# Long VectorE and GpSimd steps cut into two to four parts, and one planned duration corrected, in a planned four-layer transformer

## The chip, the core and the metric

The kernel runs on one core of a Trainium2 chip. The core has a matrix engine (TensorE, PE in the profile), three engines for elementwise work (VectorE is DVE, ScalarE is ACT, GpSimd is POOL) and a queue that starts transfers (SyncE, SP). Each engine takes its instructions strictly in the order in which the program lists them, and waits for other engines at semaphores. The metric is the device time of one execution in microseconds (us); lower is better.

## The reference

An input of 16 sequences of 256 tokens with 128 features passes through four layers in fp32. Every layer adds an attention and then a feed-forward block to x, each behind a layer norm:

```
x = x + attn_l(layernorm(x));  x = x + ffn_l(layernorm(x))       # l = 0..3
L0 attn: 16 heads of 64, l2-normed q and k, distance bias, 2 null keys;  ffn: gelu, 512 hidden
L1 attn: q of 16 heads of 8, one shared k and v, causal;  ffn: silu(x w1) * (x w2), two gelu layers of 512, w3
L2 attn: 16 heads of 64, no mask, biases;  ffn: 8 experts, each token goes to the one with the largest gate logit
L3 attn: 16 heads of 8, causal window of 128;  ffn: mix with the previous token, sigmoid(xr Wr) * (relu(xk Wk)^2 Wv)
```

## The kernel before

All of x stays in SBUF as eight tiles (xg), each for two batches, with tokens on the partitions. Layers run one after the other, but the work of neighbouring batches and layers is interleaved.

The order is not written by hand. The kernel records *steps* with `step(engine, p, ns, emit, r, w, m)`: p is a rank (smaller is earlier in the program's own order), ns the duration that the planner assumes, r, w and m are what the step reads, writes, and changes in place. Two steps that name the same value under m follow each other. `Plan.run` then plays the steps against a model of the engines: it starts with the engine that is free first, takes among the steps that could start within 40 ns the one with the smallest rank, and emits its instructions. A step is never interrupted, so a long one holds its engine for its whole planned duration. The planned durations thus decide the order of the instructions, but not how long they take on the chip. A step for two engines ("DP" is VectorE or GpSimd, "AD" is ScalarE or VectorE) has a planned duration for each and goes to the one that would end it earlier. Tile buffers (the homes: eight PSUM banks "t", "r", "probs", "pT" and so on) are handed out in the same run. SP's queue carries the loads of weights and expert rows, GpSimd's the scatters and gathers.

The places that matter here, with their lines:

- `layernorm` (455 to 482): statistics on VectorE (lines 464 and 465, two row blocks each), eps and power -1/2 on GpSimd (lines 469 and 436), and the application (line 477, two instructions), which in layer 0 is always on VectorE and otherwise "DP".
- `narrow_keys` (line 596): in layers 1 and 3 one GpSimd instruction spreads the keys of a batch over four masked copies.
- `narrow_out` (lines 683 to 687): the attention output of layers 1 and 3 is divided by the sums, for two halves z of the tokens, then turned on TensorE and projected.
- `feed1` (lines 1021 and 1022): two gating instructions for each of four blocks of 128 hidden features.
- `through` (lines 1111 to 1114): once, the bias of v is carried through the output matrix, in eight instructions.
- `Experts.gate` (lines 1197 to 1220): for each two batches of layer 2, the gate logits, the choice of the expert (`chosen`, six small VectorE instructions), counts on TensorE, and running sums on GpSimd (`running`, four). `place` computes each token's place in its expert's blocks; `scatter` (line 1304) writes 128 normed tokens at a time to DRAM by an indirect transfer from GpSimd's queue.
- `block`: SP loads an expert's weights (line 1316) and 128 rows (line 1317); the rows are turned on TensorE and copied out to a tile bT (lines 448 and 450), and two products, a relu (lines 1334 and 1336) and a bias follow. Experts work in two groups of four tiles of x (eight batches) each; `back` (line 1353) gathers the results once all blocks of a group are written. Layer 3 of the second eight batches can't begin before that.

The matrix products carry line 404 and the transposes line 432, those of the helpers that issue them; copies out of PSUM have line 448 on ScalarE and 450 on VectorE.

Of the kernel before, what the change touches and what calls it, by code (L numbers as in the profile page):

```python
# [12 lines left out]
ALU = mybir.AluOpType  # L13
AX = mybir.AxisListType

P = 128
# [223 lines left out]
def preln_d4_kernel(ctx: ExitStack, tc: tile.TileContext, x_in, vecs, rows, nullk, nullv,  # L240
                    wa0, wlat, wb1, wa2, wex, gatew, wa3, out):
    nc = tc.nc
    PSUM = bass.MemoryType.PSUM
    plan = Plan()
    step, get = plan.step, plan.get
# [188 lines left out]
    def rsqrt(t, n):  # L434

        nc.gpsimd.tensor_tensor(t, t, mhalf[:t.shape[0]].broadcast_to([t.shape[0], n]), ALU.pow)  # L436

    def x_of(b):
        return xg[b // 2][:, (b % 2) * 2:(b % 2) * 2 + 2, :]

    X = [plan.key(f"x{b}") for b in range(B)]
# [14 lines left out]
    def layernorm(b, p, xn, at, times=1, behind=(), eng="DP"):  # L456

        ln, x = get("ln"), x_of(b)  # L460

        def stats(e):
            for i in range(2):
                nc.vector.bn_stats(ln.t[0][:, i, :], x[:, i, :])
                nc.vector.bn_aggr(ln.t[1][:, i, :], ln.t[0][:, i, :])  # L465

        def scale(e):
            if times == 1:
                nc.gpsimd.tensor_scalar(ln.t[2], ln.t[1][:, :, 1], LN_EPS, 1.0, ALU.add, ALU.mult)  # L469
            else:  # L470
                nc.gpsimd.tensor_scalar(ln.t[2], ln.t[1][:, :, 1], 1.0 + LN_EPS, LN_EPS * LN_EPS, ALU.mult, ALU.add)
            rsqrt(ln.t[2], 2)

        def apply(e):
            for i in range(2):
                v = nc.vector if e == "DVE" else nc.gpsimd
                v.tensor_scalar(xn.t[:, (at + i) * D:(at + i + 1) * D], x[:, i, :], ln.t[1][:, i, 0:1],
                                ln.t[2][:, i:i + 1], ALU.subtract, ALU.mult)

        step("DVE", p, 788, stats, r=[X[b]], w=[ln])  # L480
        step("POOL", p, 1070, scale, m=[ln])
        step(eng, p, (520, 620) if eng == "DP" else 520 if eng == "DVE" else 620, apply, r=[X[b], ln] + list(behind), w=[xn])

    def turned(p, xn, nt, gamma=None):

# [105 lines left out]
    def narrow_keys(p, KT):  # L591

        KM = get("K")

        def keys(e):
            nc.gpsimd.tensor_tensor(KM.t[:, :, 0:256], KT.t[:, 0:256].unsqueeze(1).broadcast_to([P, 4, 256]),
                                    owner.unsqueeze(2).broadcast_to([P, 4, 256]), ALU.mult)

        step("POOL", p, 1850, keys, r=[KT, "owner"], w=[KM])
        return KM  # L600

    def narrow_unit(q, b, u, st, mask, mkey):
# [64 lines left out]
    def narrow_out(p, b, st, w_proj):  # L667

        t, o_sb, rs, oT = [get("t"), get("t")], get("small"), get("rs"), st["oT"]

        def turn(e):
            for i in range(4):
                turned_halves(t, 64 * i, oT.t[:, i * P:(i + 1) * P])

        step("PE", p, 250, turn, r=[oT], w=t, mode="S")

        def divided(e):

            o6 = o_sb.t[:, 0:256].rearrange("p (q z g h d) -> p q z g h d", q=2, z=2, g=2, h=4)
            r5 = rs.t.rearrange("p (z q g h) -> p z q g h", z=2, q=2, g=2)  # L680
            for z in range(2):
                t5 = t[z].t[:, 0:256].rearrange("p (s q g r) -> p s q g r", s=2, q=2, g=2)
                nc.vector.reciprocal(r5[:, z, :, :, 0:3], t5[:, 0, :, :, 24:27])
                nc.vector.reciprocal(r5[:, z, :, :, 3:4], t5[:, 1, :, :, 24:25])
                nc.vector.tensor_tensor(o6[:, :, z, :, 0:3, :], t5[:, 0, :, :, 0:24].rearrange("p q g (h d) -> p q g h d", d=8),
                                        r5[:, z, :, :, 0:3].unsqueeze(4).broadcast_to([P, 2, 2, 3, 8]), ALU.mult)
                nc.vector.tensor_tensor(o6[:, :, z, :, 3, :], t5[:, 1, :, :, 0:8],
                                        r5[:, z, :, :, 3:4].broadcast_to([P, 2, 2, 8]), ALU.mult)

        step("DVE", p - 7, 1060, divided, r=t, w=[o_sb], m=[rs])  # L690
        yT = get("small")

        for t2, src, dst in in_halves(p + 1, (o_sb, lambda i: o_sb.t[:, i * P:(i + 1) * P]), 2, lambda: yT.t):
            evac(p + 1, yT, t2, lambda src=src, dst=dst: (dst(), src()), 128)
        y = get("t")

        def project(e):
            for qc in range(2):
                mm(y.t[:, qc * P:(qc + 1) * P], yT.t[:, qc * P:(qc + 1) * P], w_proj)

        step("PE", p + 2, 450, project, r=[yT], w=[y], mode="P")
        add_to_x(p + 2, b, y)
# [10 lines left out]
    first, rank = {}, 0  # L713
# [290 lines left out]
    def feed1(g):  # L1004
        lo = first[1, 2 * g + 1] + 8 + 16
        x, xx = xg[g], [X[2 * g], X[2 * g + 1]]
        xn = get("r")
# [5 lines left out]
        for c in range(4):  # L1013
            pa, pb, th = get("t"), get("t"), get("sq")

            def up(e, c=c, pa=pa, pb=pb):
                mm(pa.t, wt("w1", c * P, P), xnT.t)
                mm(pb.t, wt("w2", c * P, P), xnT.t)

            def gated(e, c=c, pa=pa, pb=pb, th=th):  # L1020
                nc.vector.scalar_tensor_tensor(th.t, th.t, 1.0, pa.t, ALU.add, ALU.mult)
                nc.vector.scalar_tensor_tensor(h[c].t, pb.t, s12[:, c:c + 1], th.t, ALU.mult, ALU.mult)

            p = lo + 6 + c
            step("PE", p, 1724, up, r=[xnT, "w1", f"h2.{g - 1}"], w=[pa, pb], mode="P")
            step("ACT", p - 8, 560, lambda e, c=c, pa=pa, th=th: nc.scalar.activation(th.t, pa.t, AF.Tanh, scale=s1h[:, c:c + 1]),
                 r=[pa, "s1"], w=[th])
            step("DVE", p - 8, 1380, gated, r=[pa, pb, "s1"], m=[th], w=[h[c]])

        def layer(name, sname, src, p):  # L1030
            dst = [get("r") for _ in range(4)]
# [72 lines left out]

    bvo, bps = get("small"), get("t")

    def through(e):
        a = v_at["a2bv"][0]
        for c in range(8):
            wo = wA[:, 3072 + c * D:3072 + (c + 1) * D]  # L1110
            if c == 0:
                nc.vector.tensor_scalar(bvo.t[:, 0:D], wo, vec_sb[:, a:a + 1], None, ALU.mult)
            else:
                nc.vector.scalar_tensor_tensor(bvo.t[:, 0:D], wo, vec_sb[:, a + c:a + c + 1], bvo.t[:, 0:D], ALU.mult, ALU.add)

    step("DVE", first[2, 0] - 12, 1800, through, r=["w2"], w=[bvo])
    step("PE", first[2, 0] - 8, 224, lambda e: mm(bps.t[:, 0:D], ones, bvo.t[:, 0:D]), r=[bvo, "ones"], w=[bps], mode="P")
    step("DVE", first[2, 0] - 8, 200, lambda e: nc.vector.tensor_tensor(row("a2bo"), bps.t[:, 0:D], row("a2bo"), ALU.add), r=[bps], w=["a2bo"])  # L1118

# [48 lines left out]
    class Experts:  # L1168
# [12 lines left out]
        def gate(self, g, lo):  # L1181
# [11 lines left out]
            def chosen(e):  # L1193
# [4 lines left out]
                nc.vector.tensor_reduce(m1, l3, AX.X, ALU.max)  # L1198
                nc.vector.tensor_tensor(l3, l3, m1.unsqueeze(2).broadcast_to([P, 4, 8]), ALU.is_equal)
                nc.vector.scalar_tensor_tensor(l3, l3, -64.0, iota8.unsqueeze(1).broadcast_to([P, 4, 8]), ALU.mult, ALU.add)  # L1200
                nc.vector.tensor_reduce(m2, l3, AX.X, ALU.min)
                nc.vector.tensor_tensor(self.tile("oh")[:, a:a + 4, :], l3, m2.unsqueeze(2).broadcast_to([P, 4, 8]), ALU.is_equal)

            step("PE", lo + 7, 600, logits, r=[xnT], w=[ps], mode="P")
            oh = plan.get(None)
            step("DVE", lo + 5, 1150, chosen, r=[ps, "late"], m=[lg, self.key("oh")], w=[oh])
            pc = get("t")

            def counts(e):
# [7 lines left out]
            def running(e):  # L1217
                sofar = self.tile("sofar")
                for t in range(a, a + 4):
                    nc.gpsimd.tensor_tensor(sofar[:, t + 1, :], sofar[:, t, :], self.tile("ct")[:, 1, t, :], ALU.add)  # L1220

            step("PE", lo + 9, 300, counts, r=[oh], w=[pc], mode="P")
            ct = plan.get(None)
            step("DVE", lo + 3, 131, kept, r=[pc], w=[ct, self.key("ct")])
            step("POOL", lo + 9, 720, running, r=[ct], m=[self.key("sofar")])

        def place(self, g, lo):

# [60 lines left out]
                if last:  # L1289
                    v.tensor_copy(self.tile("owni"), own)  # L1290

            def in_parts(p, times, ops, r, m):

                todo = ops()
                for ns in times:
                    step("DVE", p, ns, lambda e: next(todo, None), r=r, m=m)

            in_parts(lo, (700, 600, 1100), blocks_of, [self.key("sofar")], [self.key("nb")])
            in_parts(lo, (600, 450, 650), places, [self.key("nb"), self.key("oh"), self.key("sofar")], [self.key("ct")])
            in_parts(lo + 1, (700, 1000, 800), owners, [self.key("ct")], [self.key("nb")])  # L1300

        def scatter(self, t, p):
            def f(e):
# [1 line left out]
                    out=ex_rows[self.part], out_offset=bass.IndirectOffsetOnAxis(ap=self.tile("idx")[:, t:t + 1], axis=0),  # L1305
                    in_=self.xn[self.lo + t // 4].t[:, (t % 4) * D:(t % 4 + 1) * D], in_offset=None)

            step("POOL", p, 980, f, r=[self.key("ct"), self.xn[self.lo + t // 4]], m=[self.key("rows")], tail=2500)

        def block(self, j, p):  # L1310
            w, xs, xsT, h, ys = get("w"), get("xs"), get("bT"), get("r"), get("bT")
# [277 lines left out]
```

## Time and profile before

| | |
|---|---|
| median of 3 runs | 2126.34 us (2121.66 to 2129.11) |
| profiled execution, its own time | 2132.18 us |
| its span, first to last instruction | 2130.5 us |
| mean granted TensorE clock | 0.982 of full speed |
| TensorE idle in 0 to 100 us | 14.8 us |
| TensorE idle in 1700 to 2100 us | 39.7 us |

Each line of the groups names a source line, an engine, an operation and its tiles with buffer numbers, then durations in ns. A line of waits says which instruction waited for which, how many us in total, how often, and the longest. In the list of instructions by time, a bracket at the end gives how long the engine had been idle before, and what ended that. A group of scores, exponentials and products of one batch in layer 0 takes some 36 us, in layer 1 some 33, in layer 2 some 34. The four layers lie at about 0 to 600, 570 to 1180, 1130 to 1770 and 1740 to 2130 us.

### The profile page before, as it was taken

To read this page: it belongs to the slowest core of one execution; us is meant where nothing else is said; L and a number is where in the kernel's file an instruction comes from. 1 tells how busy PE (TensorE), PEld (TensorE's weight loads), DVE (VectorE), ACT (ScalarE), POOL (GpSimd) and SP (SyncE) were. 2 spreads that over 40 slices of the span, in tenths; PEclk is the share of its full clock that TensorE was granted. 3 is DMA by queue.
4 is the path that set the end of the run, shared out by engine and by line. 5 is a ranking of instruction groups with operands and counts; after the bars stand their busy time and mean duration, and the time that the engine had idled before them with its cause. 6 is when DMAs were issued, how large, how long until landed. Compare 5 with 4: busy or idle time off the path is not lost.

```text
span 2130.5 us, 86226 instructions
## 1 busy us (share of the span) xinstructions
PE 2030.3 (95%) x34860; PEld 1395.8 (66%) x34860; DVE 1636.7 (77%) x6393; ACT 1660.5 (78%) x4834; POOL 1159.3 (54%) x2157
## 2 busy tenths in 40 slices
PE   7999999999999999999999999999999998998997
PEld 4667777777665444544546677777887775775665
DVE  7999999999887766667665467777676778677997
ACT  6999999998887776767766668877666778677996
POOL 7888888898842121212223346666454974227642
PEclk9999999999999999999999999999999998998999
DMA  5000000000140000000000000000442001441000
GB/s 168 2 2 2 2 2 2 2 2 3 32 61 12 2 3 3 3 3 3 3 3 1 2 4 5 7 7 18 123 122 74 22 7 45 140 146 29 15 8 18
DMA packets 60303, 59.08 MB, mean 28 GB/s; under 512 B 28016, under 2 KB 49024, under 8 KB 59904
## 3 DMA queue, kind: packets, MB, share of 16 engines
q1 hardware_dynamic: 57680, 49.33, 8.3%
q8 instruction: 274, 4.49, 0.9%
q0 software_dynamic: 2048, 4.20, 0.6%
q14 instruction: 125, 1.02, 0.2%
q10 hardware_dynamic: 176, 0.03, 0.0%
HBM read 43.32 MB, written 10.22 MB: 25 GB/s over the span
## 4 chain that ended last, share of the span: by engine, by line
PE 73%; DVE 12%; POOL 7%; ACT 6%; issue 3%; another core or an unknown queue 0%; POOLq 0%; ACTq 0%; DVEq 0%
PE t0x L404 9%; PE t4x L404 9%; PE t6x L404 8%; PE t1x L404 8%; PE t7x L404 8%; PE t3x L404 7%; PE t2x L404 7%; PE t5x L404 7%; PE t1x L432 1%; PE t5x L432 1%; PE t6x L432 1%; PE t7x L432 1%; PE t0x L432 1%; PE t4x L432 1%; PE t2x L432 1%
## 5 line engine op out<-in xcount | busy, mean ns | idle before, releaser
L469 POOL TENSOR_SCALAR ln_rs4x<-ln_mv4x 128x2 f32<-128x2 f32 x24 | 4.6, 193 | 92.1 <-DVE ln_mv4x L465 91.1
L469 POOL TENSOR_SCALAR ln_rs2x<-ln_mv2x 128x2 f32<-128x2 f32 x21 | 4.7, 224 | 82.7 <-DVE ln_mv2x L465 81.9
L469 POOL TENSOR_SCALAR ln_rs0x<-ln_mv0x 128x2 f32<-128x2 f32 x21 | 4.1, 193 | 78.1 <-DVE ln_mv0x L465 70.6
L469 POOL TENSOR_SCALAR ln_rs3x<-ln_mv3x 128x2 f32<-128x2 f32 x23 | 4.8, 210 | 70.9 <-DVE ln_mv3x L465 64.1
L502 POOL TENSOR_TENSOR x<-x,row_sb 128x256 f32<-128x256 f32 x48 | 35.0, 730 | 6.2 <-DVE row_sb L1118 3.4
L436 POOL TENSOR_TENSOR ss0x<-ss0x,mhalf 128x16 f32<-128x16 f32 x11 | 31.9, 2902 | 8.5 <-DVE ss0x L816 7.3
L469 POOL TENSOR_SCALAR ln_rs1x<-ln_mv1x 128x2 f32<-128x2 f32 x23 | 4.4, 193 | 57.0 <-DVE ln_mv1x L465 55.9
L534 POOL TENSOR_SCALAR probs4x<-probs4x,sums2x 128x256 f32<-128x256 f32 (+2 forms) x44 | 20.4, 477 | 25.3 <-PE t5x L404 16.5
L534 POOL TENSOR_SCALAR probs0x<-probs0x,sums2x 128x256 f32<-128x256 f32 (+2 forms) x40 | 19.2, 493 | 26.3 <-DVE sums2x L529 16.0
L534 POOL TENSOR_SCALAR probs0x<-probs0x,sums4x 128x256 f32<-128x256 f32 (+2 forms) x44 | 21.7, 506 | 21.2 <-DVE sums4x L529 20.9
L436 POOL TENSOR_TENSOR ss3x<-ss3x,mhalf 128x16 f32<-128x16 f32 x11 | 32.9, 2992 | 0.1
L436 POOL TENSOR_TENSOR ss1x<-ss1x,mhalf 128x16 f32<-128x16 f32 x11 | 32.8, 2986 | 0.1
L436 POOL TENSOR_TENSOR ss2x<-ss2x,mhalf 128x16 f32<-128x16 f32 x11 | 31.9, 2901 | 0.9 <-DVE sums1x L529 0.9
L436 POOL TENSOR_TENSOR ss5x<-ss5x,mhalf 128x16 f32<-128x16 f32 x10 | 30.5, 3045 | 0.2
L436 POOL TENSOR_TENSOR ss4x<-ss4x,mhalf 128x16 f32<-128x16 f32 x10 | 29.4, 2944 | 0.5 <-DVE sums1x L529 0.5
L1060 POOL TENSOR_TENSOR x<-x,sq0x 128x512 f32<-128x512 f32 x4 | 5.1, 1275 | 44.9 <-DVE sq0x L1058 44.9
L534 POOL TENSOR_SCALAR probs2x<-probs2x,sums0x 128x256 f32<-128x256 f32 (+2 forms) x44 | 19.7, 463 | 17.8 <-DVE sums1x L529 14.0
L534 POOL TENSOR_SCALAR probs2x<-probs2x,sums4x 128x256 f32<-128x256 f32 (+2 forms) x40 | 20.9, 535 | 12.3 <-DVE sums4x L529 11.9
L534 POOL TENSOR_SCALAR probs3x<-probs3x,sums3x 128x256 f32<-128x256 f32 (+2 forms) x44 | 19.8, 464 | 13.4 <-DVE sums3x L529 12.1
L621 DVE CUSTOM_DVE_ANT_0 probs2x<-t6x,mask 128x128 f32<-128x128 f32 (+1 forms) x44 | 11.9, 323 | 19.6 <-PE t2x L404 7.6
L534 POOL TENSOR_SCALAR probs5x<-probs5x,sums3x 128x256 f32<-128x256 f32 (+2 forms) x44 | 20.5, 482 | 11.9 <-DVE sums3x L529 11.8
L534 POOL TENSOR_SCALAR probs0x<-probs0x,sums0x 128x256 f32<-128x256 f32 (+2 forms) x44 | 21.7, 507 | 9.2 <-DVE sums1x L529 6.7
(5024 smaller groups left out, 10840.1 us busy)
## 6 DMA issues: line engine op xcount, KB each, us to landing
w0x<-in_wex_dram SPq DMA_DIRECT2D x16, 578.0 KB, 4.1
w1x<-in_wex_dram SPq DMA_DIRECT2D x15, 578.0 KB, 4.8
w2x<-in_wex_dram SPq DMA_DIRECT2D x15, 578.0 KB, 3.9
w_wA<-in_wa_dram SPq DMA_DIRECT2D x18, 256.0 KB, 4.6
ex_rows<-zero SPq DMA_DIRECT2D x2, 1472.0 KB, 29.2
w_wB<-in_wb_dram SPq DMA_DIRECT2D x11, 256.0 KB, 5.4
x<-in_x_dram SPq DMA_DIRECT2D x8, 256.0 KB, 6.2
ex_y<-bT1x SPq DMA_DIRECT2D x20, 64.0 KB, 3.4
```

The source lines that it names most:

```text
L404: nc.tensor.matmul(o[c], lhsT[:, c], rhs, start=start, stop=stop, **kw)
L432: nc.tensor.transpose(t[z].t[:, c:c + 64], block[r], ident[r, r])
L436: nc.gpsimd.tensor_tensor(t, t, mhalf[:t.shape[0]].broadcast_to([t.shape[0], n]), ALU.pow)
L469: nc.gpsimd.tensor_scalar(ln.t[2], ln.t[1][:, :, 1], LN_EPS, 1.0, ALU.add, ALU.mult)
L502: step("POOL", p, 670, lambda e: nc.gpsimd.tensor_tensor(x_of(b), x_of(b), row_over(name, 2), ALU.add), r=reads, m=[X[b]])
L534: nc.gpsimd.tensor_scalar(pr.t[:, j, a:z], pr.t[:, j, a:z], sums.t[:, i:i + 1], 1.0, ALU.mult, ALU.mult)
L621: nc.vector.tensor_tensor_reduce(pr.t[:, g % 2, c], s[g].t[:, c], m, -1.0, 3.0e38, ALU.add, ALU.min, nm.t[:, j:j + 1])
L1060: step("POOL", lo + 30, 1300, lambda e: nc.gpsimd.tensor_tensor(x, x, ys.t.rearrange("p (c d) -> p c d", d=D), ALU.add), r=[ys, "w1"], m=xx)
```

## The change

A helper `in_parts` takes a generator in place of a function, and records one step for each of several durations; each step emits the instructions up to the generator's next yield. It existed inside `place` and is now shared. These steps are cut with it: the norm's statistics (two parts, one row block each), the keys (two parts, and two instructions of half the size in place of one), the division (two, one for each half z), the gating (two), the bias row (four), the choice (three) and the running sums (two). Two planned durations change as well: the norm's application on GpSimd from 620 to 1640 ns, and the scatter from 980 to 1100. Apart from the keys no instruction's shape changes; the planner may place others between the parts.

```diff
+    def in_parts(eng, p, times, ops, r=(), w=(), m=()):
+        todo = ops()
+        for ns in times:
+            step(eng, p, ns, lambda e: next(todo, None), r=r, w=w, m=m)
...
-        step("DVE", p, 788, stats, r=[X[b]], w=[ln])
+        in_parts("DVE", p, (400, 400), stats, r=[X[b]], m=[ln])
         step("POOL", p, 1070, scale, m=[ln])
-        step(eng, p, (520, 620) if eng == "DP" else 520 if eng == "DVE" else 620, apply, r=[X[b], ln] + list(behind), w=[xn])
+        step(eng, p, (520, 1640) if eng == "DP" else 520 if eng == "DVE" else 620, apply, r=[X[b], ln] + list(behind), w=[xn])
...
-        def keys(e):
-            nc.gpsimd.tensor_tensor(KM.t[:, :, 0:256], KT.t[:, 0:256].unsqueeze(1).broadcast_to([P, 4, 256]),
-                                    owner.unsqueeze(2).broadcast_to([P, 4, 256]), ALU.mult)
-        step("POOL", p, 1850, keys, r=[KT, "owner"], w=[KM])
+        def keys():
+            for h in (0, 2):
+                nc.gpsimd.tensor_tensor(KM.t[:, h:h + 2, 0:256], KT.t[:, 0:256].unsqueeze(1).broadcast_to([P, 2, 256]),
+                                        owner[:, h:h + 2].unsqueeze(2).broadcast_to([P, 2, 256]), ALU.mult)
+                yield
+        in_parts("POOL", p, (990, 990), keys, r=[KT, "owner"], w=[KM])
...
-        step("DVE", p - 7, 1060, divided, r=t, w=[o_sb], m=[rs])
+        in_parts("DVE", p - 7, (530, 530), divided, r=t, w=[o_sb], m=[rs])
...
-            step("DVE", p - 8, 1380, gated, r=[pa, pb, "s1"], m=[th], w=[h[c]])
+            in_parts("DVE", p - 8, (690, 690), gated, r=[pa, pb, "s1"], m=[th], w=[h[c]])
...
-    step("DVE", first[2, 0] - 12, 1800, through, r=["w2"], w=[bvo])
+    in_parts("DVE", first[2, 0] - 12, (720,) * 4, through, r=["w2"], m=[bvo])
...
-            step("DVE", lo + 5, 1150, chosen, r=[ps, "late"], m=[lg, self.key("oh")], w=[oh])
+            in_parts("DVE", lo + 5, (430, 400, 400), chosen, r=[ps, "late"], m=[lg, self.key("oh")], w=[oh])
...
-            step("POOL", lo + 9, 720, running, r=[ct], m=[self.key("sofar")])
+            in_parts("POOL", lo + 9, (510, 510), running, r=[ct], m=[self.key("sofar")])
...
-            step("POOL", p, 980, f, r=[self.key("ct"), self.xn[self.lo + t // 4]], m=[self.key("rows")], tail=2500)
+            step("POOL", p, 1100, f, r=[self.key("ct"), self.xn[self.lo + t // 4]], m=[self.key("rows")], tail=2500)
```

More of the change, by code (lines that the diff above doesn't have):

```diff
@@ L460, in layernorm, with stats @@
         ln, x = get("ln"), x_of(b)
-        def stats(e):
+        def stats():
             for i in range(2):
@@ L593, in narrow_keys @@
         KM = get("K")
[L595 to L599 removed]
+        def keys():
+            for h in (0, 2):
+                nc.gpsimd.tensor_tensor(KM.t[:, h:h + 2, 0:256], KT.t[:, 0:256].unsqueeze(1).broadcast_to([P, 2, 256]),
+                                        owner[:, h:h + 2].unsqueeze(2).broadcast_to([P, 2, 256]), ALU.mult)
+                yield
+        in_parts("POOL", p, (990, 990), keys, r=[KT, "owner"], w=[KM])
         return KM
@@ L675, in narrow_out, with divided @@
         step("PE", p, 250, turn, r=[oT], w=t, mode="S")
-        def divided(e):
+        def divided():
             o6 = o_sb.t[:, 0:256].rearrange("p (q z g h d) -> p q z g h d", q=2, z=2, g=2, h=4)
@@ L688, in divided @@
                                         r5[:, z, :, :, 3:4].broadcast_to([P, 2, 2, 8]), ALU.mult)
-        step("DVE", p - 7, 1060, divided, r=t, w=[o_sb], m=[rs])
+                yield
+        in_parts("DVE", p - 7, (530, 530), divided, r=t, w=[o_sb], m=[rs])
         yT = get("small")
@@ L1018, in up, with gated @@
                 mm(pb.t, wt("w2", c * P, P), xnT.t)
-            def gated(e, c=c, pa=pa, pb=pb, th=th):
+            def gated(c=c, pa=pa, pb=pb, th=th):
                 nc.vector.scalar_tensor_tensor(th.t, th.t, 1.0, pa.t, ALU.add, ALU.mult)
+                yield
                 nc.vector.scalar_tensor_tensor(h[c].t, pb.t, s12[:, c:c + 1], th.t, ALU.mult, ALU.mult)
@@ L1105, in preln_d4_kernel, with through @@
     bvo, bps = get("small"), get("t")
-    def through(e):
+    def through():
         a = v_at["a2bv"][0]
@@ L1114, in through @@
                 nc.vector.scalar_tensor_tensor(bvo.t[:, 0:D], wo, vec_sb[:, a + c:a + c + 1], bvo.t[:, 0:D], ALU.mult, ALU.add)
-    step("DVE", first[2, 0] - 12, 1800, through, r=["w2"], w=[bvo])
+            if c % 2:
+                yield
+    in_parts("DVE", first[2, 0] - 12, (720,) * 4, through, r=["w2"], m=[bvo])
     step("PE", first[2, 0] - 8, 224, lambda e: mm(bps.t[:, 0:D], ones, bvo.t[:, 0:D]), r=[bvo, "ones"], w=[bps], mode="P")
@@ L1191, in logits, with chosen @@
                     mm(ps.t[:, i * 8:(i + 1) * 8], xnT.t[:, i * P:(i + 1) * P], gw_sb)
-            def chosen(e):
+            def chosen():
                 l3 = lg.t[:, 0:32].rearrange("p (c e) -> p c e", e=8)
@@ L1198, in chosen @@
                 nc.vector.tensor_reduce(m1, l3, AX.X, ALU.max)
+                yield
                 nc.vector.tensor_tensor(l3, l3, m1.unsqueeze(2).broadcast_to([P, 4, 8]), ALU.is_equal)
                 nc.vector.scalar_tensor_tensor(l3, l3, -64.0, iota8.unsqueeze(1).broadcast_to([P, 4, 8]), ALU.mult, ALU.add)
+                yield
                 nc.vector.tensor_reduce(m2, l3, AX.X, ALU.min)
@@ L1215, in kept, with running @@
                 nc.vector.tensor_copy(self.tile("ct")[:, :, a:a + 4, :], pc.t[:, 0:64].rearrange("p (k c e) -> p k c e", k=2, c=4))
-            def running(e):
+            def running():
                 sofar = self.tile("sofar")
@@ L1220, in running @@
                     nc.gpsimd.tensor_tensor(sofar[:, t + 1, :], sofar[:, t, :], self.tile("ct")[:, 1, t, :], ALU.add)
+                    if t == a + 1:
+                        yield
             step("PE", lo + 9, 300, counts, r=[oh], w=[pc], mode="P")
@@ L1290, in owners @@
                     v.tensor_copy(self.tile("owni"), own)
[L1292 to L1300, printed above, removed]
+            in_parts("DVE", lo, (700, 600, 1100), blocks_of, r=[self.key("sofar")], m=[self.key("nb")])
+            in_parts("DVE", lo, (600, 450, 650), places, r=[self.key("nb"), self.key("oh"), self.key("sofar")], m=[self.key("ct")])
+            in_parts("DVE", lo + 1, (700, 1000, 800), owners, r=[self.key("ct")], m=[self.key("nb")])
         def scatter(self, t, p):
```

## The prediction

> **What bounds the kernel now.** I read the page's totals and slices first, then the stretches of equal length, then TensorE's waits, and last the queue of GpSimd around the longest of them.
>
> ```profile
> span 2130.5 us, 86226 instructions
> PE 2030.3 (95%) x34860; PEld 1395.8 (66%) x34860; DVE 1636.7 (77%) x6393; ACT 1660.5 (78%) x4834; POOL 1159.3 (54%) x2157
> PE 73%; DVE 12%; POOL 7%; ACT 6%; issue 3%; another core or an unknown queue 0%; POOLq 0%; ACTq 0%; DVEq 0%
> ```
>
> TensorE is busy 95% of the span and holds 73% of the chain that ended last. No engine that this change touches carries a fifth of that chain. Only 100 us of TensorE's span are idle, so the question is where they lie (columns: stretch, length, PE, PEld, DVE, ACT, POOL busy, granted clock, DMA share, GB/s):
>
> ```profile
> 200.00:300.00 100.00, 99.14 (x1452) 71.10 (x1450) 95.31 (x358) 93.95 (x283) 86.67 (x165) 1.00 0.01 2
> 900.00:1000.00 100.00, 98.95 (x1863) 48.88 (x1856) 73.19 (x318) 71.69 (x161) 20.60 (x27) 1.00 0.01 3
> 1300.00:1400.00 100.00, 99.70 (x1428) 77.62 (x1426) 72.41 (x196) 77.24 (x256) 60.48 (x124) 1.00 0.02 5
> 1800.00:1900.00 100.00, 84.78 (x2442) 65.75 (x2434) 69.11 (x345) 67.43 (x208) 31.41 (x53) 0.95 0.50 149
> 2000.00:2100.00 100.00, 94.13 (x2349) 65.86 (x2344) 93.52 (x514) 97.11 (x265) 45.47 (x73) 0.97 0.04 11
> ```
>
> In the midst of layers 0, 1 and 2 (first three rows) TensorE has about 1 us idle in 100; what VectorE or GpSimd do there is covered. From 1700 us on it is idle for some 50 us, and the granted clock lies between 0.90 and 0.97 in each stretch of 100. First (1800 to 1900) the second group of experts starts; later (2000 to 2100) ScalarE and VectorE are full. A change on VectorE and GpSimd is worth something only there. The waits between 1796 and 1824 us:
>
> ```profile
> PE t7x L404 <- ACT bT2x L448: 3.2, 1, 3.2
> PE t5x L432 <- DMA xs2x<-ex_rows: 1.6, 1, 1.6
> PE t2x L432 <- DVE small1x L687: 1.0, 1, 1.0
> ```
>
> The first expert block's rows (xs2x) come late, then ScalarE copies them late. Why they come late is seen in GpSimd's queue:
>
> ```profile
> 1790.87 0.97 POOL L1304 DMA_INDIRECT ex_rows<-r7x,idx1x  x1 [1.40 <-DMA ex_rows<-r7x,idx1x]
> 1796.78 1.89 POOL L596 TENSOR_TENSOR K2x<-q2x,owner 128x1024 f32<-128x1024 f32 x1 [4.94 <-ACT q2x L1418]
> 1799.51 0.19 POOL L469 TENSOR_SCALAR ln_rs1x<-ln_mv1x 128x2 f32<-128x2 f32 x1 [0.84 <-DVE ln_mv1x L465]
> 1799.78 0.72 POOL L436 TENSOR_TENSOR ln_rs1x<-ln_rs1x,mhalf 128x2 f32<-128x2 f32 x1
> 1800.70 1.06 POOL L1304 DMA_INDIRECT ex_rows<-r7x,idx1x  x1 [0.19 <-issue]
> ```
>
> The last scatter stands behind a key step that waited 4.94 us for ScalarE and behind a norm's scale.
>
> **The change part by part.** The built orders of both kernels give the counts.
>
> *Norms applied.* The new price (1640 for 620) takes GpSimd out of 23 norms: 46 of its instructions go to VectorE. By the rows of line 477, one takes 797 ns on GpSimd and 343 ns on VectorE:
>
> ```profile
> L477 POOL TENSOR_SCALAR r4x<-x,ln_mv2x,ln_rs2x x6: 787/798/807, 797.9 to 1427.0; 128x128 f32<-128x128 f32 x6
> L477 DVE TENSOR_SCALAR r0x<-x,ln_mv0x,ln_rs0x x4: 317/341/463, 8.1 to 307.3; 128x128 f32<-128x128 f32 x4
> ```
>
> GpSimd loses 46 x 0.797 = 36.7 us, VectorE gains 46 x 0.343 = 15.8 us. In layer 1 lie 28 of them, from its fifth batch on, and 8 in layer 2: TensorE covers both (99 of 100 us; VectorE at 73 gains about 2 in 100). Without that cover each norm would cost 0.69 us of VectorE, 12.4 us for the 18. Layer 3 has 10 (3.4 us); the last 4 of them fall behind the experts, where VectorE and ScalarE are full and share the evictions. They cost between 0 and 4 x 0.343 = 1.4; I take half, +0.7. An earlier norm saves TensorE at most what it now waits for line 477 outside start and end, 1.0 us: I take -0.5.
>
> [...]
>
> *Keys.* 32 instructions of 1.895 us become 64. Half of one is 0.95 in proportion; the nearest row is line 1466 with two inputs of 512 elements, 1.042. So a batch costs 0 to 0.19 more on GpSimd; nearest is line 1466, +0.19. TensorE has no wait listed that a key step ended, and GpSimd stands idle before it (4.94 above), so this is 0; if each of the last 8 batches lay open it would be 1.5. In one batch only does something stand between the halves.
>
> *Division, gating, choice, statistics, the bias row, running sums.* The instructions stay the same, so their time is 0; what changes is what gets between. In 31 of 32 divisions one to four VectorE instructions now stand between the halves, mostly a mask-and-maximum pair of 0.35 us per row block, so the attention output comes 0.3 to 0.7 us later. TensorE's waits for it (line 687) sum to about 5.5 us in layer 3. The turning of it is moved back too (behind eight more transposes in many batches), so I take +0.5 out of 0 (all filled) to 16 x 0.35 = 5.6. Gating is parted in 17 of 32, in layer 1, under TensorE: 0. Of 128 statistics 45 are parted, most under TensorE. The bias row (8 x 352 ns) is at 987 us, covered.
>
> *The last group's rows.* From choice to index there are 60 VectorE instructions instead of 62, so the index is as early as before: no cost. On GpSimd the order is now: scatter, scatter, keys, scatter, scale, a copy of V (0.76), an apply (2 x 0.80), scatter. The copy and the apply were behind the last scatter before, so it starts 2.3 us later, at about 1803. On SP's queue the load of xs2x stands behind it, and loads of the next two blocks behind that one. But TensorE's order puts 60 more matmuls ahead of that block (32 products, 8 of the output projection, some transposes), about 2 us of work that now fills idle time; and the copy of bT2x, which made TensorE wait 3.2 us, is not held by the rows: ScalarE came to it at 1809.63, behind 16 exponentials. They still stand before it, with three more copies of 0.48, so it comes 1.4 us later. The block thus starts between 2 us earlier (all filled) and 2.3 later (none). I take half of ScalarE's 1.4, +0.7, because its queue ended the longer wait.
>
> *The order as a whole.* TensorE changes its array tiling 658 times instead of 653. At 2102.45 a change put 0.16 us between starts that are otherwise 0.06 apart: 5 x 0.1 = +0.5, with 0 to 0.9 as ends. The planner's new costs reorder nearly everything after 100 us, which no row prices directly. Between 1980 and 2100 us TensorE's busy time in 20 us goes from 17.5 to 19.6: a random step of about 1 us in each of the 20 stretches after 1740 us makes some 4.5 us either way. The sum takes 0 for it, the range 9 (twice that).
>
> All 32 key steps last 1891 to 1912 ns, whether VectorE is busy for 66 or 94% of its stretch: work moved to VectorE does not lengthen GpSimd's. [...]
>
> Sum: +0.7 - 0.5 + 0 + 0.5 + 0.7 + 0.5 = +1.9. The profiled execution took 2132.18 (span 2130.5, 1.7 around it) and would take 2134.1. That execution stands 5.8 above the median 2126.34 of the three runs, which becomes 2128.2: I say 2128.
>
> **Rivals.**
> - *Slower: the second experts start late.* Place: the last scatter. If the 2.3 us pass whole to the end, and the blocks behind it, whose rows and weights are fetched into three buffers, lose a half-clock stretch on the way, it decides. From 1800 to 1820 the clock was 0.83, which is 3.4 us of work lost. Price 2.3 + 3.4 in place of 0.7 makes the sum +6.9; with the divisions at 5.6 in place of 0.5, +12: 2133 to 2138. It decides from some 6.4 us on. For it: TensorE idle for 6.4 of these 20 us. Against: 60 matmuls now fill it.
> - *Faster: the plan fits the chip.* With true prices nothing arrives later than TensorE was told. Waits of TensorE for VectorE and GpSimd after 1740 us sum to about 20 us; halving them gives -10, and a clock stretch less -3: 2115. For it: the old prices were wrong by 1 us for 67 norms. Against: TensorE waited almost nowhere for line 477, so that error was hidden.
> - *Nothing seen:* all is filled, within the 0.3% (6.4 us) that measurements of this kernel can tell; the three runs alone spread by 7.4 us.
>
> **How the numbers follow.** The likeliest case is my sum with the random part: chance 0.45, own range 2119 to 2137 (9 either way). The slower rival gets 0.29, the faster 0.26. The bound of 0.3% lies at 2120 and 2132.7. Of my own case 0.33 falls within, 0.04 below, 0.08 above; the faster rival gives 0.22 below and 0.04 within, the slower 0.26 above and 0.03 within. So faster 0.26, same 0.40, slower 0.34. The range for 8 in 10 reaches to both rivals: 2113 to 2143 (the rivals' ends, 2115 and 2138, and a part of the random step beyond each).
>
> **What would show it.** Right: line 477's successor 104 times on VectorE and 88 on GpSimd; layers 0 to 2 with TensorE at 97% or more and the same length; the last scatter at 1802 to 1804 with an apply ahead of it; the wait for bT2x's copy under 3 us; 2000 to 2100 us with ScalarE above 95%. Wrong: a stretch before 1700 us that changes by over 3 us, or a second-expert stage that ends more than 4 us away from before. The prediction fails if the random reordering is worth more than 9 us, most likely through half-clock stretches after 1740 us.

## The result and the profile after

The changed kernel takes 2143.27 us (median of 5 runs, 2140.37 to 2144.54) and the kernel before, beside it, 2124.35 (5 runs, 2121.58 to 2129.11): a ratio of 1.0081, with a 95% interval from 1.0064 to 1.0098. So it is 17 us slower. The forecast was 2128, with "same" (within 0.3%) the likeliest; the result is slower than that bound and lies at the very end of the range (0.3 us past 2143), on the side of the slower rival. What follows shows that this rival's reason was not the main one.

The page's totals, after:

```profile
span 2142.6 us, 86224 instructions
PE 2032.7 (95%) x34852; PEld 1403.1 (65%) x34852; DVE 1650.6 (77%) x6438; ACT 1667.3 (78%) x4835; POOL 1125.9 (53%) x2143
```

GpSimd lost 33 us of work and VectorE gained 14, near the forecast 36.7 and 15.8. TensorE has the same share. The totals don't show the loss, so the same stretches of 100 us come next (columns as in the prediction):

```profile
200.00:300.00 100.00, 98.85 (x1428) 70.10 (x1430) 94.52 (x355) 91.39 (x277) 88.12 (x173) 1.00 0.01 2
900.00:1000.00 100.00, 97.13 (x1780) 49.80 (x1776) 66.36 (x320) 74.45 (x177) 14.38 (x21) 0.98 0.01 3
1300.00:1400.00 100.00, 99.02 (x1382) 77.74 (x1384) 75.77 (x197) 80.51 (x274) 65.32 (x133) 1.00 0.02 5
1800.00:1900.00 100.00, 83.12 (x2323) 64.18 (x2326) 71.19 (x361) 64.05 (x183) 33.67 (x56) 0.93 0.44 136
2000.00:2100.00 100.00, 93.31 (x2383) 65.95 (x2374) 95.17 (x514) 97.30 (x264) 50.97 (x89) 0.97 0.04 11
```

The row of 900 to 1000 stands out: in layer 1 TensorE got through 1780 matmuls, where it was 1863 before, though it is idle for only 1.8 us more. A stretch of 100 us is no whole number of batches, so this is only a hint; but layer 1 repeats itself every two batches, and such periods can be compared. These are the stretches from one addition of an attention output to x to the one two batches later; first before, then after, for the same 1228 matmuls:

```profile
819.34:884.53 65.19, 64.66 (x1228) 32.34 (x1224) 44.55 (x202) 46.07 (x105) 13.41 (x17) 1.00 0.01 3
```

```profile
818.10:886.78 68.68, 66.71 (x1228) 34.49 (x1224) 43.87 (x198) 49.08 (x114) 8.98 (x13) 0.98 0.01 3
955.41:1023.30 67.89, 65.85 (x1228) 33.99 (x1224) 45.91 (x204) 49.10 (x114) 10.61 (x15) 1.00 0.01 2
```

A period takes 2.7 to 3.5 us longer. Of that, 1.4 to 1.5 us are idle time of TensorE (0.53 before, 1.97 and 2.04 after). Another 1.2 us are the same matmuls keeping it busy for longer at full clock (64.66 against 65.85). In the first of the two, whose granted clock is 0.98, it is busy for 0.9 us more still. ScalarE has nine instructions more per period: in the built order of layer 1, ScalarE does 177 of the copies of 512 columns out of PSUM and VectorE 120, where it was 157 and 140. TensorE's waits between 750 and 1100 us sum to 2.5 us before and 8.7 after. The longest after are:

```profile
PE t7x L432 <- DVE pT2x L456: 1.0, 2, 0.6
PE t0x L404 <- DVE rs1x L693: 0.9, 3, 0.3
PE t0x L432 <- DVE r7x L456: 0.6, 1, 0.6
PE t2x L432 <- DVE r8x L456: 0.6, 1, 0.6
```

Most are transposes (line 432) that wait for a copy on VectorE (line 456). What VectorE did while one of these waits ended, at 870.47 us, and after it, in the list of its instructions by time:

```profile
869.73 0.69 DVE L456 COPY pT0x<-t7x 128x512 f32<-128x512 f32 x1
870.34 0.68 DVE L1031 SCALAR_TENSOR_TENSOR sq0x<-sq0x,t2x 128x512 f32<-128x512 f32 x1
870.93 0.68 DVE L1031 SCALAR_TENSOR_TENSOR sq1x<-sq1x,t3x 128x512 f32<-128x512 f32 x1
871.53 0.74 DVE L1033 SCALAR_TENSOR_TENSOR r0x<-t4x,s,sq0x 128x512 f32<-128x512 f32 x1
872.19 0.74 DVE L1033 SCALAR_TENSOR_TENSOR r1x<-t0x,s,sq1x 128x512 f32<-128x512 f32 x1
```

Two gating blocks are interleaved: first part of one, first part of the next, then both second parts. Before, sq0 was followed by its own r, then sq1 by its own:

```profile
866.06 0.75 DVE L1022 SCALAR_TENSOR_TENSOR r0x<-t3x,s,sq0x 128x512 f32<-128x512 f32 x1
866.73 0.68 DVE L1021 SCALAR_TENSOR_TENSOR sq1x<-sq1x,t7x 128x512 f32<-128x512 f32 x1
867.51 0.75 DVE L1022 SCALAR_TENSOR_TENSOR r5x<-t1x,s,sq1x 128x512 f32<-128x512 f32 x1
```

To place the whole difference, I cut each run at four additions of an attention output to x (the 15th, 33rd, 47th and 64th). The table gives the lengths of these stretches in the profiled execution, in us, and in the last column what the ratio of the timed runs makes of the kernel before's median (with its interval):

| run | layer 0 | layer 1 | layer 2 | layer 3 | difference by runs |
|---|---|---|---|---|---|
| before | 587.9 | 590.4 | 563.0 | 377.1 | |
| changed kernel | 589.9 | 600.5 | 562.9 | 376.8 | +17.2 (13.6 to 20.8) |
| gated_alone | 586.3 | 603.7 | 564.0 | 373.0 | +13.6 (9.4 to 17.6) |
| gated_on_gpsimd | 587.7 | 603.6 | 564.1 | 370.5 | +10.6 (7.4 to 13.8) |
| gated_no_lag | 587.6 | 591.0 | 567.4 | 363.9 | -1.9 (-4.9 to 1.1) |
| moved_alone | 586.2 | 592.3 | 563.3 | 375.4 | +2.6 (0.2 to 5.1) |
| price_alone | 586.1 | 589.4 | 562.4 | 371.7 | -1.9 (-4.5 to 0.6) |
| stats_alone | 588.5 | 591.6 | 562.2 | 364.8 | -1.9 (-5.3 to 1.5) |
| gated_whole | 588.7 | 595.1 | 562.9 | 376.3 | +13.0 (8.7 to 17.4) |
| all_no_lag | 589.3 | 594.1 | 567.5 | 365.2 | +7.7 (4.7 to 10.6) |
| division_alone | 588.5 | 605.0 | 563.9 | 357.8 | +7.9 (5.3 to 10.4) |
| division_no_lag | 585.4 | 590.6 | 565.9 | 354.4 | -7.4 (-9.8 to -4.9) |
| no_lag_statistics_whole | 586.8 | 592.3 | 563.6 | 357.4 | -7.6 (-10.2 to -5.1) |
| gating_and_division_whole | 584.9 | 589.2 | 556.6 | 364.8 | -13.6 (-18.9 to -8.1) |

Between before and the changed kernel, layer 1 takes 10.1 of the 11.7 us that the profiled executions differ by up to the last addition. The execution profiled of before was 7.8 us above the median of these five runs, which is why the difference by runs is larger than that of the profiles. price_alone has the very same order of TensorE and was profiled at its median: it reached the last addition 8.8 us sooner than before, and against it the changed kernel loses 3.8 us in layer 0, 11.1 in layer 1, 0.5 in layer 2 and 5.1 in layer 3. From the 47th addition on, TensorE has the same order in before, price_alone, moved_alone, gated_alone and gated_on_gpsimd, and these five executions take 370.5 to 377.1 us there, before the longest. So some 6 us in the last column of lengths are no effect of an order. The last four kernels of the table ran beside a median of 2121.60 for the kernel before and the others beside 2124 to 2127, so their ratios are to be compared, not their times.

### The profile page after: what moved, and what is told of

It is laid out like the page before. It is cut to its first block, busy times and chain, and to the rows that moved or that the text cites. A ratio compares the mean times of both kernels' runs of the same rounds, so it can differ in the third digit from the quotient of the medians.

```text
span 2142.6 us, 86224 instructions
## 1 busy us (share of the span) xinstructions
PE 2032.7 (95%) x34852; PEld 1403.1 (65%) x34852; DVE 1650.6 (77%) x6438; ACT 1667.3 (78%) x4835; POOL 1125.9 (53%) x2143
## 5 line engine op out<-in xcount | busy, mean ns | idle before, releaser
L541 POOL TENSOR_SCALAR probs2x<-probs2x,sums0x 128x256 f32<-128x256 f32 (+2 forms) x44 | 19.7, 463 | 22.3 <-DVE sums0x L536 15.5
L541 POOL TENSOR_SCALAR probs2x<-probs2x,sums6x 128x256 f32<-128x256 f32 (+2 forms) x44 | 19.6, 461 | 16.7 <-DVE sums6x L536 16.3
L541 POOL TENSOR_SCALAR probs2x<-probs2x,sums2x 128x256 f32<-128x256 f32 (+2 forms) x44 | 21.2, 494 | 12.3 <-DVE sums2x L536 8.3
L541 POOL TENSOR_SCALAR probs4x<-probs4x,sums6x 128x256 f32<-128x256 f32 (+2 forms) x40 | 17.7, 455 | 18.1 <-DVE sums6x L536 10.7
```

The costliest lines, as they stand in the source:

```text
L541: nc.gpsimd.tensor_scalar(pr.t[:, j, a:z], pr.t[:, j, a:z], sums.t[:, i:i + 1], 1.0, ALU.mult, ALU.mult)
```

## The experiments

**Which part does it.** Four kernels: before with one part of the change, or the changed kernel with one part undone.

gated_alone is before with the gating in two parts (helper included):

```diff
-            step("DVE", p - 8, 1380, gated, r=[pa, pb, "s1"], m=[th], w=[h[c]])
+            in_parts("DVE", p - 8, (690, 690), gated, r=[pa, pb, "s1"], m=[th], w=[h[c]])
```

> The kernel before with the gating alone in two parts. Its built order is that of before up to layer 1; in layer 1 VectorE gets 22 more norm applications and ScalarE 13 more of the large copies out of PSUM, as a by-product of the new order. Theory 1 (the parted gating spoils the order of layer 1): two batches of layer 1 take 67 to 69 us instead of 65.2, TensorE waits for copies out of PSUM, and the end comes 8 to 15 us later, 2132 to 2139. Theory 2 (the new price of the application and the applications it moves are the cause): layer 1 as before, within 3 us of the kernel before. Theory 3 (any reordering costs some random time, mostly in layer 3): layer 1 as before, the end off by up to 8 us either way.

Measured: ratio 1.0064 (1.0044 to 1.0083), and layer 1 is 13.3 us longer. A period:

```profile
817.44:885.27 67.83, 65.86 (x1228) 33.99 (x1224) 43.74 (x199) 48.63 (x113) 8.66 (x11) 1.00 0.01 3
```

The whole loss of layer 1 is there with this part alone, as theory 1 expected, and outside layer 1 TensorE's order is that of before. (2139.71 us is 0.7 above that theory's range.)

gated_whole is the changed kernel with the gating as one step again:

```diff
-            in_parts("DVE", p - 8, (690, 690), gated, r=[pa, pb, "s1"], m=[th], w=[h[c]])
+            step("DVE", p - 8, 1380, gated, r=[pa, pb, "s1"], m=[th], w=[h[c]])
```

> The changed kernel with the gating in one step again. Theory 1: two batches of layer 1 return to 65 to 66 us; what stays is the 4 us that come up at 120 to 235 us and whatever layer 3 makes of its own order: 2128 to 2135, thus 8 to 15 us less than the changed kernel. Theory 2: it stays slower by 12 us or more, 2138 to 2146. Theory 3: layer 1 unchanged at 68.6 us for two batches, the end anywhere.

Measured: ratio 1.0061 (1.0041 to 1.0082). At 2138.10 us, theory 1 missed: it expected 2128 to 2135. The gating does not explain everything: without it, 13 us are still there by runs, and layer 1 is still 4.7 us longer than before. The time fits theory 2, but price_alone below rules out its reason.

stats_alone is before with the statistics in two parts:

```diff
-        step("DVE", p, 788, stats, r=[X[b]], w=[ln])
+        in_parts("DVE", p, (400, 400), stats, r=[X[b]], m=[ln])
```

> The kernel before with the statistics alone in two parts. It is the only part of the change that reaches layer 0, whose order is here that of the changed kernel. Theory 1: the 4 us that the changed kernel loses between 120 and 235 us appear here too, and layer 1, whose TensorE order is that of before, keeps 65.2 us for two batches: 2128 to 2134. Theory 2: no loss in layer 0, within 2 us. Theory 3: as theory 1 in layer 0, with up to 8 us either way from layer 3.

Measured: ratio 0.9991 (0.9975 to 1.0007). Between the third and the fifth addition (158 to 231 us) it is 3.6 us longer, as is every kernel here with statistics in parts (75.7 or 75.8 for 72.1), and 2.4 of it are given back before layer 0 ends. It costs nothing by runs; theory 1 had expected 2128 to 2134, and 2125.62 came.

price_alone is before with the new price of the application:

```diff
-        step(eng, p, (520, 620) if eng == "DP" else 520 if eng == "DVE" else 620, apply, r=[X[b], ln] + list(behind), w=[xn])
+        step(eng, p, (520, 1640) if eng == "DP" else 520 if eng == "DVE" else 620, apply, r=[X[b], ln] + list(behind), w=[xn])
```

> The kernel before with the new planned durations of the norm's application alone. TensorE's order is that of before throughout; two norms in sum go from GpSimd to VectorE. Theory 1: within 2 us of the kernel before, in every layer. Theory 2 (the price and what it moves cost the time): 6 to 12 us slower. Theory 3: within 2 us, since nothing is reordered on TensorE.

Measured: ratio 0.9991 (0.9979 to 1.0003). In its built order, only 4 instructions go to VectorE, not 46. The other 42 moved for other reasons: the gating in parts alone moves 24.

**Why the gating in parts costs.** The planner lets a step end a tail after its duration (95 ns on VectorE) and lets another step see it 60 ns later. It applies this between two parts on the same engine too. When the first part is over, the second is 155 ns from being ready, more than the 40 ns within which rank decides, so any other ready step goes between. gated_no_lag takes that time away for all steps in parts:

```diff
-        for ns in times:
-            step(eng, p, ns, lambda e: next(todo, None), r=r, w=w, m=m)
+        for i, ns in enumerate(times):
+            step(eng, p, ns, lambda e: next(todo, None), r=r, w=w, m=m, tail=-plan.SEEN[eng] if i + 1 < len(times) else None)
```

> Before, with the gating alone in two parts, but the first part of a step (in the helper for parts) gets a tail of -60 (VectorE) or -110 (GpSimd), so that the planner lets the second part follow at once; 165 changed matters only to the planner. Theory A (the planner charges 95 + 60 = 155 ns between two parts on one engine, so it puts the first half of the next block between them, holds four PSUM banks at once and moves copies to ScalarE): layer 1's order of TensorE is again that of before, two batches take 65.2 us there (68.5 with the gating alone), and the time is before's within 5 us: 2121 to 2131. Theory B (any parting of the gating costs, by what else gets between the parts): two batches take 68 us or more, the time is 2136 to 2144. Theory C (the 22 norm applications of layer 1 that moved to VectorE with the gating in parts cost it): they stay on GpSimd here mostly, so by C too the time comes back to 2121 to 2131; the two runs that follow tell A from C.

Measured: ratio 0.9991 (0.9977 to 1.0005). In the built order none of the 32 gatings has anything between its parts (18 have with the lag), and TensorE's order in the steady part of layer 1 is before's, matmul for matmul. A period:

```profile
819.63:884.82 65.19, 64.67 (x1228) 32.34 (x1224) 44.55 (x202) 46.03 (x105) 13.37 (x17) 1.00 0.01 3
```

Every number of before is back: 65.19, 64.67, 32.34, 44.55. The difference between the two plans of the same parts is 15.5 us by runs (13.6 + 1.9). Two limits: the mended plan leaves no gating parted at all, so it shows that the lag parts them and that this order costs, but not that every order with something between would cost (theory B is not excluded). And the helper also serves the parts inside `place`, whose order changes with it; layer 2 becomes 4.4 us longer.

**Or is it the norms that moved to VectorE?** moved_alone is before with the 32 norms of layer 1 put on VectorE (shown for its attention; its feed-forward likewise); gated_on_gpsimd is gated_alone with the same norms put on GpSimd ("POOL" in place of "DVE"):

```diff
-        layernorm(b, lo, xn, 0)
+        layernorm(b, lo, xn, 0, eng="DVE")
```

> Before, with all 32 norm applications of layer 1 put on VectorE and nothing in parts; TensorE's order is that of before. Theory A (TensorE covers them, VectorE is busy 73% there): two batches take 65.2 to 65.7 us in layer 1, time within 4 us of before: 2122 to 2130. Theory C (the moved applications cost the 3.4 us for two batches): 68 us or more, 2134 to 2142.

> The gating alone in two parts, lag as changed, with all norm applications of layer 1 kept on GpSimd; TensorE's order in layer 1 is that of the run with the gating alone. Theory A: two batches still take 67.5 to 69 us, time 2134 to 2143. Theory C: 65.2 to 66 us, 2121 to 2131.

Measured: 1.0012 (1.0001 to 1.0024) and 1.0050 (1.0035 to 1.0065). A period of the first, then of the second:

```profile
819.07:884.41 65.34, 64.74 (x1228) 32.34 (x1224) 45.97 (x209) 46.07 (x105) 8.64 (x11) 1.00 0.01 3
```

```profile
818.50:887.14 68.64, 66.66 (x1228) 34.60 (x1224) 40.81 (x190) 49.11 (x114) 15.01 (x19) 0.98 0.01 3
```

VectorE works 1.4 us more per period in the first and TensorE loses 0.15. In the second VectorE has 3.7 us less to do than before, and TensorE loses 3.45. So theory C falls: the load of VectorE is not it, the order is (TensorE's order is that of gated_alone here, step for step). moved_alone's 2130.63 us lies 0.6 above theory A's range, 3.4 under theory C's. The new order differs on all engines at once, and no run separates TensorE's own sequence from the copies that went to ScalarE.

**The rest: division, statistics, and everything without lag.**

all_no_lag is the changed kernel with the mended helper.

> The changed kernel whole, with the same mending of the lag between parts for every step in parts. Theory A: layer 1 falls back to 65.2 us for two batches; what remains is some 3 us in layer 0 (the statistics in parts stay apart in the order) and the scatter of the last layer: 2120 to 2134. Theory B: 2138 to 2146, as the changed kernel.

Measured: 1.0036 (1.0022 to 1.0050). Periods of layer 1 are 65.19 us again, and 9.5 us of the 17.2 are gone, but the kernel stays slower than before by 7.7; 2132.98 is just within what theory A expected. 44 of the 128 statistics are still parted. In the changed kernel something stands between the two parts of 57 (the prediction's 45 is a miscount), so for most of them the lag doesn't decide.

division_alone is before with the division in two parts, division_no_lag the same with the mended helper:

```diff
-        step("DVE", p - 7, 1060, divided, r=t, w=[o_sb], m=[rs])
+        in_parts("DVE", p - 7, (530, 530), divided, r=t, w=[o_sb], m=[rs])
```

> Before with the division alone in two parts, the planner's 155 ns between them. What it tells: whether the 12 us that the changed kernel keeps when the gating is whole again are the division's. Theory A (the lag between parts spoils the order of layer 1 here too): layer 1 becomes 5 to 8 us longer, as it is with the gating whole, and the time is 2130 to 2140. Theory D (those 12 us are the other parts and what the last layer makes of a new order): layer 1 within 2 us of before, time 2121 to 2131.

> The division alone in two parts, with the lag between parts mended as before (tail -60 or -110). TensorE's order in layer 1 is that of before. Theory A: layer 1 as before within 1 us, time 2120 to 2131, and under that of the division alone by what that lost in layer 1. If the two are equal, the lag does not matter for the division.

Measured: 1.0037 (1.0025 to 1.0049) and 0.9965 (0.9954 to 0.9977). The first period of the stretch, with and then without the lag (the first has 1240 matmuls between its ends):

```profile
824.65:892.09 67.44, 65.96 (x1240) 33.46 (x1232) 44.61 (x201) 47.09 (x109) 11.83 (x15) 1.00 0.01 3
```

```profile
817.09:882.27 65.18, 64.66 (x1228) 32.33 (x1224) 44.53 (x203) 46.05 (x105) 13.37 (x17) 1.00 0.01 3
```

Layer 1 is 14.6 us longer with the lag, twice what theory A expected, and 0.2 longer without. With the lag 30 of 32 divisions have something between their parts, without it one. gated_whole has 30 parted divisions too and loses only 4.7 us in layer 1, so the price of a parted step depends on the rest of the plan. In layer 3 both kernels are 13 to 23 us faster than the five executions with before's order there, which I did not expect of either; so 2129.56 falls just under theory A's range and 2113.08 well under.

gating_and_division_whole is the changed kernel with both of these as one step again (the two diffs above, reversed):

> The changed kernel with gating and division whole again: statistics, keys, bias row, choice and running sums in parts, the new prices. TensorE's order in layer 1 is that of before. Theory A: 3 to 4 us more in layer 0 (the statistics), nothing in layer 1; 2121 to 2133. If these parts cost by themselves (theory D): 2134 to 2141.

Measured: 0.9936 (0.9911 to 0.9962), 2108.03 us for 2121.60 beside it. It is below what both theories expected, and faster than both kernels of this case. Layer 1 is as before (65.18 a period). Against price_alone the gain lies in layer 2 (5.9 us shorter) and layer 3 (6.9). So taking back the two partings alone is worth 30.8 us to the changed kernel (17.2 + 13.6).

no_lag_statistics_whole is the changed kernel with the mended helper and whole statistics (the diff of stats_alone, reversed):

> The changed kernel with the lag mended (2132.98 by runs) and the statistics whole again. If the statistics in parts are what is left over before (3.5 us in layer 0, and 5 us up to layer 1's start): layer 0 equals before and the time is 2124 to 2130. If their loss in layer 0 is given back later, as the run with the statistics alone suggests: 2130 to 2136.

Measured: 0.9964 (0.9952 to 0.9976), that is 15 us under all_no_lag, far more than the 3.5 to 5 that theory gave to the statistics. Layer 0 gives 2.5 of that, layer 1 1.8, layer 2 3.9 and layer 3 7.9. But stats_alone and gating_and_division_whole have statistics in parts, and are no slower than before. So it isn't a price of the statistics; it depends on what they meet.

What stays open: why an order is good or bad behind layer 1. Over the runs of the table that have layer 1 within 4 us of before, the time goes from -13.6 to +7.7 us, with layer 3 from 354 to 375, far more than the 6 us between executions of one order. No single part of the change goes along with it. I found no wait that explains it, and did not test one.

## Where the prediction held and where it failed, point by point

That the time lies at the end of the range is luck: the range reached that far for a late start of the second experts and for random steps after 1740 us, and the largest loss is in layer 1, which the prediction called covered.

- **"Gating is parted in 17 of 32, in layer 1, under TensorE: 0."** This step failed. The count was right, the price is 13.6 us by itself (4.2 of the 17.2 when only the gating is taken back, and 30.8 with the division). "TensorE covers both (99 of 100 us ...)" is true of work that is added beside TensorE: moved_alone puts 38 more instructions of layer 1 on VectorE at 0.15 us a period. It is not true of the order. When the planner parts the gating, it also hands out PSUM banks and copies otherwise and writes TensorE's own program anew. The busy share of 99% covered the added work here, and said nothing of a worse sequence.
- **Division, "+0.5 out of 0 ... to 5.6".** I priced the delay of the attention output in layer 3. By itself the division cost 7.9 by runs, with +14.6 in layer 1, while layer 3 was 13 to 19 us shorter than in the executions with before's order there. That I looked only at layer 3 is the same error.
- **Norms applied: "the new price ... takes GpSimd out of 23 norms".** The count of the whole change was right and its cause wrong. The price moves 2 norms. That the move is nearly free was right.
- **"The order as a whole: ... the sum takes 0 for it, the range 9."** The size is roughly right for the kernels that have layer 1 as before (-13.6 to +7.7 by runs; -13.6 lies beyond it). I allowed such steps only after 1740 us, where TensorE visibly waits. The sign named as "wrong", a stretch before 1700 us that changes by over 3 us, came: layer 1, +10.1, and 158 to 231 us, +3.6. The +0.5 for the array's tiling was not tested.
- **Keys, statistics, bias row, choice, running sums: 0.** gating_and_division_whole has them all and loses nothing in layer 1. For the statistics, 3.6 us are lost at 158 to 231 us and 2.4 regained. As a fixed price the 0 holds for stats_alone (-1.9) and fails between all_no_lag and no_lag_statistics_whole (15 us); 57 of them are parted, not 45.
- **"The last group's rows", +0.7.** Right in size, and the 2.3 us of the scatter did not come. The last scatter has the apply and the copies of V ahead of it, as forecast, and starts 59.0 us after the 47th addition (59.3 before), not 2.3 later. The load of the first block's rows starts 62.2 us after it for 61.65: 0.6 later. "The wait for bT2x's copy under 3 us" is right only by name: the 3.2 us are gone, but TensorE stands 5.05 us before the product that reads bT2x, where 1.59 (for the rows) and 3.24 were before. That product starts 69.3 us after the 47th addition (68.5 before), 0.8 later.

```profile
1810.58 1.59 POOL L484 TENSOR_SCALAR r11x<-x,ln_mv2x,ln_rs2x 128x128 f32<-128x128 f32 x2
1812.35 1.11 POOL L1315 DMA_INDIRECT ex_rows<-r6x,idx1x  x1 [0.18 <-issue]
```

- **The slower rival, "the second experts start late".** Its sign was right; its mechanism is not what cost most. The last scatter is not late, and most of the loss was there before the experts began. From the 47th addition to the last, the changed kernel takes 376.8 us and before 377.1, but the other four executions of before's order take 370.5 to 375.4: 1 to 6 us lost in this stage are not ruled out, and no run says what they would be.
- **The faster rival, "the plan fits the chip".** The true price of the application alone changed nothing (price_alone). Both new prices with the parts that leave layer 1 as it was did give -13.6, near its -11, but the runs do not show that truer prices are the reason.

## What to carry to other kernels

Where a planner writes the order, cutting one step can reorder every engine: read the new order of the engine that is the bound, stage by stage, before calling a change covered, and give a changed steady period a price even where the bound is 99% busy. A planner that charges a hand-over between two parts of one step on the same engine will often put something between them (18 of 32 gatings, 30 of 32 divisions here); decide whether that is wanted. Test parts one at a time and in groups, since what they are worth together (+17.2) is no sum of what they are worth alone.

## What the hardware showed

**Two dependent operations on VectorE did not follow as closely as two independent ones: 0.78 against 0.60 us from start to start.** The same gating instructions, in gated_no_lag and then in gated_alone (columns: start in us, duration, then the instruction):

```profile
865.57 0.68 DVE L1027 SCALAR_TENSOR_TENSOR sq0x<-sq0x,t0x 128x512 f32<-128x512 f32 x1
866.35 0.75 DVE L1029 SCALAR_TENSOR_TENSOR r1x<-t3x,s,sq0x 128x512 f32<-128x512 f32 x1
867.02 0.68 DVE L1027 SCALAR_TENSOR_TENSOR sq1x<-sq1x,t7x 128x512 f32<-128x512 f32 x1
867.80 0.75 DVE L1029 SCALAR_TENSOR_TENSOR r5x<-t1x,s,sq1x 128x512 f32<-128x512 f32 x1
```

```profile
870.27 0.68 DVE L1027 SCALAR_TENSOR_TENSOR sq0x<-sq0x,t2x 128x512 f32<-128x512 f32 x1
870.87 0.68 DVE L1027 SCALAR_TENSOR_TENSOR sq1x<-sq1x,t3x 128x512 f32<-128x512 f32 x1
871.47 0.74 DVE L1029 SCALAR_TENSOR_TENSOR r4x<-t1x,s,sq0x 128x512 f32<-128x512 f32 x1
```

A second part that reads the first's result starts 0.78 us after it; an independent instruction starts 0.60 after one of the same length (0.68 us): the difference is 0.18 us. Not all pairs are alike: in before, whose gatings are whole, 24 of the 32 start 0.76 to 0.79 us apart and eight 0.71 to 0.72. So the planner's lag of 155 ns is about true for these pairs (0.11 to 0.19), and interleaving the two blocks shown saves VectorE some 0.36 us (twice 0.18). It was still a loss, in the order of all engines that came with it.

**A stretch at half clock behind 1.07 us of waiting among transposes.** Around the two waits for copies in layer 1, in steps of 1 us (after):

```profile
868.00:869.00 1.00, 0.53 (x11) 0.25 (x5) 0.98 (x3) 1.00 (x3) 0.00 (x0) 1.00 0.00 0
869.00:870.00 1.00, 0.87 (x16) 0.70 (x16) 0.85 (x2) 1.00 (x3) 0.00 (x0) 1.00 0.03 8
870.00:871.00 1.00, 0.53 (x15) 0.53 (x15) 1.00 (x3) 0.37 (x1) 0.00 (x0) 0.98 0.00 0
871.00:872.00 1.00, 1.00 (x38) 0.89 (x37) 1.00 (x3) 0.79 (x2) 0.00 (x0) 0.50 0.00 0
```

TensorE is idle for 1.07 us of these first three and then runs at half clock for about 3.4 us (0.50 in each stretch from 871 to 874, 0.81 in the next). From 867.55 us to the drop it did almost nothing but transposes; the half clock falls on the products behind them. A stretch with more idle time kept the full clock: before is busy for only 1.89 of the 3.41 us from 1110.20 on, 1.05 of them with products, and its clock stays at 1.00. What brings the half clock, and whether transposes have a part in it, no run here tests.

**Busy for longer without a slower clock.** In the disturbed layer 1, the same 1228 matmuls keep TensorE busy 1.2 us longer per period at a granted clock of 1.00. Four score products on separate row groups, each 0.69 us long, started at 836.30, 836.31, 836.32 and 836.43 us before, and at 836.26, 836.27, 836.53 and 836.72 in gated_alone: spread over 0.46 us in place of 0.13, so they ran less side by side. That this is the whole 1.2 us is not shown.
